# Down projections with tile 2's activations in two slots, the residual added by VectorE, and probability splits placed behind the next exponentials

## The chip, the cores and the metric

The kernel runs on one core of a Trainium2 chip. The metric is the device time of one execution in microseconds (us), lower being better; several executions are timed and their median is compared.

The core has engines that each work through their own instructions in order: TensorE (PE in the profile, with its weight loads as PEld), VectorE (DVE), ScalarE (ACT), GpSimd (POOL) and SyncE (SP), which here only starts DMA transfers. They wait for each other by semaphores.

## The reference

A block of four layers is applied to x of shape (2, 1024, 512) in fp32, each with a layer norm ahead of it and x added after it:

```python
x = x + attn_a(layernorm(x))
x = x + ffn(layernorm(x))
x = x + attn_b(layernorm(x))
x = x + ffn(layernorm(x))
```

attn_a is a chunked linear attention with 4 heads of 128 and chunks of 128; the change does not touch it. attn_b is a softmax attention of one head of width 512, without a mask, over 2 batches of 1024 rows, with weights W_q, W_k, W_v, W_o:

```python
scores = einsum('bqe,bke->bqk', Q, K) / sqrt(512)
out = einsum('bqk,bke->bqe', softmax(scores), V) @ W_o
```

ffn has a hidden width of 1408. Its weights are integers, W = (wq - 128) * scale per output column, and it computes `qlinear(silu(qlinear(x, gate)) * qlinear(x, up), down)`. Both ffn layers use the same weights.

## The kernel before

The 2048 rows of x are 16 tiles of 128 rows. A group is 4 tiles, so 512 rows. All matmuls are to be nearly as exact as fp32. For this, operands are split into a high part (rounded by a copy on ScalarE) and a low part (source minus high part, mostly on VectorE): `split`, lines 83 to 86, with the copy in L85 and the subtraction in L86. A product is then two or three matmuls of these parts that add up in PSUM (L96 to L98 in `mm3`).

The four layers run one after another: attention A, the ffn called "f" (L777), attention B, and the ffn called "g" (L959). What the next layer needs at its start (layer norm of its first groups, sums of operands for its first products) is done in steps that are placed among the work of the layer before.

**The ffn** (lines 670 to 775) runs in two halves, `pr` = 0 and 1, of 8 tiles each. In a half, a loop runs over the 11 blocks of 128 hidden columns, `j`. The gate and up products of the half's two groups are made by a Strassen scheme with seven block products instead of eight (`products`, L304, P1 to P7); their sums are put together on ScalarE and VectorE, and `finish` (L695 to L718) applies silu, multiplies gate by up, and writes the hidden activations: tiles 0 and 1 into a work tile `sg`, tiles 2 and 3 into `ha`, tiles 4 to 7 into `hb`. `finish` of block j is written after the first four products of block j+1; that of the last block stands behind the loop. `finish` also splits the block's part of tiles 0 and 1 into their `hs` tiles (128x128 elements; the subtraction is VectorE's in f's first half and for the last block, GpSimd's otherwise). An `hs` tile holds both parts of one row tile's whole hidden activation, 128 x 2 x 1408; they come from a pool with two buffers, so tile 2 can be split only when the projection of tile 0 has read its own, tile 3 when that of tile 1 has, and so on.

Behind the loop over j come the **down projections** of the 8 tiles, `i` = 0 to 7 (L747 to L775). Step i splits tile i+1 (L752, in two parts of 6 and 5 blocks, 768 and 640 elements wide), loads x of the tile into `xr` (SyncE, L754), makes 22 matmuls of 128x128 by 128x512, by turns with the high part (L761) and the low part (L762) of each hidden block, multiplies by the scale of the columns (VectorE, L763), adds x (L765, on GpSimd; on VectorE for the very last tile, which goes in two halves), and stores the tile (SyncE, L769). Then two of the side steps for the next half or layer are placed, ordered behind the last split of this step. At i = 4 the first half also loads the first two weight blocks of the second half (`stationary`, L775); the third follows when the next half begins. Weight blocks and the operands of the products lie in a pool "slots" of 12 tiles of 128 x 2048 (L39, function `slot`). A half has eleven weight blocks, made three ahead, and a slot is free again when the seven products of its block are done.

**Attention B** (lines 788 to 956) goes over the tiles `t` of queries. `scores_b` makes the scores in two PSUM tiles (psc), takes their maximum on VectorE (L829, with L832 and L833 to form `nm`), exponentials on ScalarE (L838, into `pe`, with their sum), and the reciprocal of the sum (`ri`, VectorE, L848 and L849). `probs_T` transposes the exponentials: VectorE transposes within blocks of 32 (L871), the result is stored to DRAM (L873), and four loads (L881) bring it back in transposed order to `ptl`. Then L884 to L886 split it in two parts, high parts into `pth`, low parts in place. Only for the last tile, t = 15, PE makes the transposes instead (ppt, L866), and their PSUM result is split at once. `out_b` makes 24 matmuls with the split V (pob, L96 to L98), scales by `ri` and adds x (L897), and stores (L898). The loop at the end of the stage calls, for each i, side steps, `scores_b` of i+1, `probs_T` of i, and `out_b` of i-1; after the loop it makes the first two weight blocks of ffn g and then `out_b` of tile 15.

**What sets the order.** The program is written in the order above, but the framework schedules it: a planner simulates the program and gives each engine its order, within the dependences and within edges that the kernel states. `behind(...)` states such edges: what is placed inside comes, on its own engine, after the instructions named. The list `last` holds the latest tile's two exponentials and reciprocal. A change of an edge or of an engine can therefore also move instructions far from the edited lines.

Of the kernel before, what the change touches and what calls it, by code (L numbers as in the profile page):

```python
# [10 lines left out]
F32R = mybir.dt.float32r  # L11
I32 = mybir.dt.int32
AF = mybir.ActivationFunctionType
ALU = mybir.AluOpType
AX = mybir.AxisListType

P = 128
# [7 lines left out]
KH = HID // P  # L25
ST = 4
# [8 lines left out]
def hybrid_block_kernel(ctx: ExitStack, tc: tile.TileContext, a, out):  # L35
    nc = tc.nc
# [12 lines left out]
    def slot(name, dt=F32R):  # L49

        return wp.tile([P, 2048], dt, tag="slot", name=name)
# [24 lines left out]
    def behind(inss):  # L76

        es = ExitStack()
        for ins in inss:
            es.enter_context(tc.issue_after(ins))  # L80
        return es

    def split(hi, lo, src, eng=None):

        c = nc.scalar.copy(hi, src)  # L85
        return c.ins, (eng or nc.vector).tensor_tensor(lo, src, hi.bitcast(F32), ALU.subtract).ins  # L86
# [583 lines left out]
    def ffn(src, dst, nm, wcs, after):  # L670


        with ExitStack() as fctx:
            fh = fctx.enter_context(tc.tile_pool(name=f"ffnh{nm}", bufs=1))
            f1 = fctx.enter_context(tc.tile_pool(name=f"ffn1{nm}", bufs=2))
            fw = fctx.enter_context(tc.tile_pool(name=f"ffnw{nm}", bufs=KH))
            fp = fctx.enter_context(tc.tile_pool(name=f"ffn{nm}", bufs=4))
            wd = []
            for pr in range(2):
                if pr == 0:  # L680
                    early = ln_steps(src, nm, 2) + ln_steps(src, nm, 3)
                    late = combine(nm, 1)
                else:
                    early, late = (list(x) for x in after)

                ha = fh.tile([P, 2, KH, P], F32, tag="ha", name=f"ha{nm}{pr}")
                hb = fh.tile([P, ST, KH, P], F32, tag="hb", name=f"hb{nm}{pr}")
                hs = {}

                def h_split(i, js, src, eng):  # L690
                    if i not in hs:
                        hs[i] = f1.tile([P, 2, KH, P], F32R, tag="hs", name=f"hs{nm}{pr}_{i}")
                    return split(hs[i][:, 0, js], hs[i][:, 1, js], src, eng)

                def finish(j, w, X, Z, V, up):  # L695

                    products(X, w, nm, pr, "P2", False)
                    products(Z, w, nm, pr, "P3", False)
                    products(V, w, nm, pr, "P4", False)
                    tiles = lambda x: x.rearrange("p (i c) -> p i c", c=P)  # L700
                    su = su_s[:, j : j + 1]
                    sg = fp.tile([P, 512], F32, tag="sg", name=f"sg{nm}{pr}_{j}")
                    nc.scalar.activation(sg, X, AF.Silu, scale=sg_s[:, j : j + 1])
                    nc.scalar.activation(hb[:, :, j], tiles(Z), AF.Silu, scale=sg_s[:, j : j + 1])
                    h01 = sg[:, 0:256]
                    nc.vector.scalar_tensor_tensor(h01, V[:, 0:256], su, h01, ALU.mult, ALU.mult)
                    nc.vector.scalar_tensor_tensor(
                        ha[:, :, j], tiles(V[:, 256:512]), su, tiles(sg[:, 256:512]), ALU.mult, ALU.mult
                    )
                    nc.vector.scalar_tensor_tensor(hb[:, :, j], tiles(up), su, hb[:, :, j], ALU.mult, ALU.mult)  # L710
                    for i in range(2):
                        done = h_split(
                            i,
                            j,
                            h01[:, i * P : (i + 1) * P],
                            None if j == KH - 1 or (nm == "f" and pr == 0) else nc.gpsimd,
                        )
                    return done  # L718

                begun = None  # L720
                for j in range(KH):
                    for n in range(len(wcs), min(j + 3, KH)):
                        wcs.append(stationary(n, f"{nm}{pr}", (xp, "xres") if nm == "f" and pr == 0 else None))
                    w = wcs[j]
                    X, Y, Z, V = (psum(f"p{n}{nm}{pr}_{j}") for n in "XYZV")
                    for ps, n in ((X, "P1"), (Y, "P6"), (Z, "P5"), (V, "P7")):
                        products(ps, w, nm, pr, n, True)
                    u2 = fp.tile([P, 512], F32, tag="sg", name=f"u2{nm}{pr}_{j}")
                    nc.scalar.copy(u2, X)  # L729
                    nc.vector.tensor_tensor(u2, Y, u2, ALU.add)  # L730
                    up = fp.tile([P, 512], F32, tag="sg", name=f"up{nm}{pr}_{j}")
                    nc.scalar.copy(up, Z)
                    nc.vector.tensor_tensor(Z, Z, u2, ALU.add)
                    nc.vector.tensor_tensor(V, V, u2, ALU.add)
                    nc.vector.tensor_tensor(up, V, up, ALU.add)  # L735
                    if begun:
                        finish(*begun)
                    begun = j, w, X, Z, V, up
                    for _ in range((1, 1, 1, 1, 2, 2, 1, 1, 1, 1, 2)[j] if early else 0):
                        early.pop(0)()  # L740
                    if pr == 0:
                        d = fw.tile([P, 512], F32R, tag="wd", name=f"wd{nm}{j}")
                        nc.sync.dma_start(out=d.bitcast(F32), in_=wd_d[j])
                        wd.append(d)
                done = finish(*begun)
                wcs = []
                for i in range(2 * ST):  # L747
                    t = pr * 2 * ST + i
                    if 1 <= i < 2 * ST - 1:
                        n = i + 1  # L750
                        for js in (slice(0, 6), slice(6, KH)):
                            done = h_split(n, js, ha[:, n - 2, js] if n < ST else hb[:, n - ST, js], None)  # L752
                    xr = xp.tile([P, D], F32, tag="xres", name=f"xr{nm}{t}")
                    nc.sync.dma_start(out=xr, in_=src[t])  # L754
                    o = fp.tile([P, 512], F32, tag="sg", name=f"o{nm}{t}")

                    last = nm == "g" and t == NT - 1
                    for ds in [slice(0, 256), slice(256, 512)] if last else [slice(0, 512)]:
                        ps = psum(f"po{nm}{t}_{ds.start}")[:, ds]
                        for j in range(KH):  # L760
                            nc.tensor.matmul(ps, hs[i][:, 0, j], wd[j][:, ds], start=j == 0, stop=False)  # L761
                            nc.tensor.matmul(ps, hs[i][:, 1, j], wd[j][:, ds], start=False, stop=j == KH - 1)  # L762
                        nc.vector.tensor_tensor(o[:, ds], ps, sd_b[:, ds], ALU.mult)  # L763
                        add = nc.vector if last else nc.gpsimd
                        add.tensor_tensor(xr[:, ds], o[:, ds], xr[:, ds], ALU.add)  # L765
                        if last:
                            nc.sync.dma_start(out=dst[t][:, ds], in_=xr[:, ds])
                    if not last:
                        nc.sync.dma_start(out=dst[t], in_=xr)  # L769
                    with behind(done):  # L770
                        for _ in range(2 if i > 0 else 0):
                            if early or late:
                                (early or late).pop(0)()
                    if pr == 0 and i == 4:
                        wcs = [stationary(n, f"{nm}1") for n in range(2)]  # L775
# [12 lines left out]
    with ExitStack() as bctx:  # L788
# [3 lines left out]
        for dst, d, n in ((wm, m_d, "wm"), (wvo, vo_d, "wvo")):  # L792
            two = [slot(f"{n}{m}") for m in range(2)]
# [58 lines left out]
        def probs_T(b, i):  # L852
# [4 lines left out]
            if t == NT - 1:  # L857

                lo = bp.tile([P, NK, P], F32R, tag="ptl", name=f"ptl{t}")
                hi = bp.tile([P, NK, P], F32R, tag="pth", name=f"pth{t}")  # L860
                for s in range(2):
                    ps = psum(f"ppt{t}_{s}").rearrange("p (k c) -> p k c", k=4)
                    ks = slice(s * 4, s * 4 + 4)
                    for k in range(4):
                        n = (s * 4 + k) * P
# [10 lines left out]
            lo = bp.tile([P, NK, P], F32R, tag="ptl", name=f"ptl{t}")  # L876
            hi = bp.tile([P, NK, P], F32R, tag="pth", name=f"pth{t}")
            raw = lo.bitcast(F32)
            placed = p_d[i].rearrange("k (c j) (r q) -> r j (k c) q", c=4, r=4)
            for r in range(4):  # L880
                nc.sync.dma_start(  # L881
                    out=raw[32 * r : 32 * (r + 1)].rearrange("p k (c q) -> p (k c) q", c=4), in_=placed[r]
                )
            for s in range(2):  # L884
                ks = slice(s * 4, s * 4 + 4)
                split(hi[:, ks], lo[:, ks], raw[:, ks])  # L886
            ptT[t] = hi, lo, ri

        def out_b(b, i):
# [132 lines left out]
```

## Time and profile before

| | |
|---|---|
| time, median of 3 runs | 997.01 us (995.41 to 999.16) |
| profiled execution | 995.43 us |
| its span in the trace | 993.7 us |
| mean clock of TensorE | 0.991 of full |
| busy: PE, DVE, ACT, POOL | 955.3, 681.8, 374.2, 269.0 us |
| L765 on GpSimd, ffn f and g | 16 of 25.0 us in all, 15 of 24.4 us in all |
| matmuls L761 and L762, f | 176 and 176 |
| matmuls L761 and L762, g | 187 and 187 |

The profile is of one execution. The span runs from its first instruction to its last; the execution's own time lies a little above it. Times are in microseconds from the span's start; "ns" is said where it is meant. A group's row names line, engine, operation, output, inputs, sizes and count; after the first bar stand busy time and mean length in ns, after the second the idle time of that engine just before these instructions, and what ended most of it. A row of the timeline starts with the start and the length of one instruction or of several that follow each other, and ends with the wait ahead of it in brackets. The letters f, g and b at the end of names stand for the two ffn layers and for attention B: `hsf`, `pof` and `xrf` are hs, the projection's PSUM tile and xr of ffn f. Successive matmuls of 512 columns start 0.227 us apart at full clock; a matmul's own length in the rows is longer, since they overlap.

### The profile page before, as it was taken

What the parts mean: (1) busy time and instruction counts of PE and PEld (TensorE: products, weight loads), DVE (VectorE), ACT (ScalarE), POOL (GpSimd) and SP (SyncE); (2) the same over time, 40 slices, a digit from 0 to 9 for tenths busy, and PEclk for the clock granted to TensorE, in tenths of its full rate; (3) what the DMA queues carried; (4) which work ended last, traced back from release to release, by engine and by line L of the source; (5) the groups of instructions that cost most, each with busy time, mean ns of one, the idle gap of its engine ahead of it and who ended that gap; (6) DMA issues with size and microseconds to landing.
All of it is one profiled execution on the core that took longest, in us unless ns stands there. A gap on an engine that the chain in (4) does not pass through costs nothing.

```text
span 993.7 us, 13137 instructions
## 1 busy us (share of the span) xinstructions
PE 955.3 (96%) x4450; PEld 786.8 (79%) x4450; DVE 681.8 (69%) x1294; ACT 374.2 (38%) x719; POOL 269.0 (27%) x345
## 2 busy tenths in 40 slices
PE   8999999988898999999999999999997999999998
PEld 6788888877776777887888888888876888788877
DVE  7666858779876699786526556356667775976665
ACT  4653334233665433443222223222223443444421
POOL 4442314253634133212200411205501111321122
PEclk9999999999999999999999999999998999999999
DMA  8536364564797555652704767328668762464112
GB/s 271 200 104 174 124 156 140 142 180 158 253 350 229 148 202 205 185 146 75 264 22 88 163 162 168 98 64 190 165 151 271 250 175 44 152 235 153 38 53 96
DMA packets 219250, 160.06 MB, mean 161 GB/s; under 512 B 154992, under 2 KB 170672, under 8 KB 219184
## 3 DMA queue, kind: packets, MB, share of 16 engines
q1 hardware_dynamic: 217136, 155.03, 52.3%
q0 software_dynamic: 2048, 4.20, 2.0%
q8 instruction: 35, 0.57, 0.2%
q14 instruction: 31, 0.25, 0.1%
HBM read 102.66 MB, written 41.84 MB: 145 GB/s over the span
## 4 chain that ended last, share of the span: by engine, by line
PE 56%; DVE 2%; SPq 2%; DMA 1%; ACT 1%; issue 1%; POOL 0%; ACTq 0%; DVEq 0%
PE pZg L304 4%; PE pXg L304 4%; PE pVg L304 4%; PE pog L762 4%; PE pog L761 4%; PE psc L96 3%; PE psc L98 3%; PE pob L96 3%; PE psc L97 3%; PE pob L97 3%; PE pob L98 3%; PE pYg L304 2%; PE pof L762 2%; PE pof L761 2%; PE pqb L97 1%; PE pqb L96 1%
## 5 line engine op out<-in xcount | busy, mean ns | idle before, releaser
L762 PE MATMUL pof<-wdf,hsf 128*128 128x512 f32 x176 | 68.3, 392 | 4.3 <-DVE hsf L86 4.3
L762 PE MATMUL pog<-wdg,hsg 128*128 128x512 f32 (+1 forms) x187 | 69.0, 378 | 3.0 <-DVE hsg L86 3.0
L761 PE MATMUL pog<-wdg,hsg 128*128 128x512 f32 (+1 forms) x187 | 69.1, 378 | 0.0
L761 PE MATMUL pof<-wdf,hsf 128*128 128x512 f32 x176 | 68.1, 391 | 0.0
L96 PE MATMUL pob<-vh,pth 128*128 128x512 f32 x128 | 50.8, 397 | 0.0
L96 PE MATMUL psc<-xh_b,qh 128*128 128x512 f32 x128 | 50.5, 395 | 0.0
L98 PE MATMUL psc<-xh_b,ql 128*128 128x512 f32 x128 | 50.5, 395 | 0.0
L97 PE MATMUL psc<-xT_b,qh 128*128 128x512 f32 x128 | 50.5, 394 | 0.0
L97 PE MATMUL pob<-vl,pth 128*128 128x512 f32 x128 | 50.5, 394 | 0.0
L98 PE MATMUL pob<-vh,ptl 128*128 128x512 f32 x128 | 50.4, 394 | 0.0
L304 PE MATMUL pXf<-B_f,wcf 128*128 128x512 f32 x176 | 47.0, 395 | 3.3 <-ACT u2f L729 2.2
L86 POOL TENSOR_TENSOR hsg<-sgg,hsg 128x128 fp32r<-128x128 f32 x40 | 17.6, 460 | 117.6 <-ACT hsg L85 95.4
L304 PE MATMUL pVf<-T_f,wcf 128*128 128x512 f32 x176 | 46.6, 391 | 1.4 <-DVE upf L735 0.7
L304 PE MATMUL pXg<-B_g,wcg 128*128 128x512 f32 x176 | 47.2, 389 | 0.0
L304 PE MATMUL pVg<-T_g,wcg 128*128 128x512 f32 x176 | 46.7, 389 | 0.0
L85 ACT CAST pth<-ptl 128x512 fp32r<-128x512 f32 x30 | 17.1, 619 | 75.9 <-DMA ptl<-p 64.0
L765 POOL TENSOR_TENSOR xrf<-of,xrf 128x512 f32<-128x512 f32 x16 | 25.0, 1562 | 75.3 <-DVE of L763 61.4
L838 ACT ACTIVATE pe<-psc,nm 128x512 f32<-128x512 f32 x32 | 21.7, 684 | 58.6 <-DVE nm L833 58.6
L762 PEld LDWEIGHTS pog<-wdg,hsg 128*128 128x128 f32 x187 | 35.1, 188 | 10.0 <-DVE hsg L86 3.6
L762 PEld LDWEIGHTS pof<-wdf,hsf 128*128 128x128 f32 x176 | 33.1, 188 | 12.6 <-DVE hsf L86 5.8
L304 PEld LDWEIGHTS pXf<-B_f,wcf 128*128 128x128 f32 x176 | 32.3, 188 | 12.8 <-ACT u2f L729 4.0
L765 POOL TENSOR_TENSOR xrg<-og,xrg 128x512 f32<-128x512 f32 x15 | 24.4, 1624 | 61.5 <-DVE og L763 48.7
(288 smaller groups left out, 2667.7 us busy)
## 6 DMA issues: line engine op xcount, KB each, us to landing
wcg<-wc SPq DMA_DIRECT2D x22, 896.0 KB, 5.8
wc<-wcf SPq DMA_DIRECT2D x11, 896.0 KB, 4.5
wcf<-wc SPq DMA_DIRECT2D x11, 896.0 KB, 4.8
p<-py SPq DMA_DIRECT2D x15, 512.0 KB, 3.0
ptl<-p SPq DMA_DIRECT2D x60, 128.0 KB, 3.0
xin_a<-in_x SPq DMA_DIRECT2D x16, 256.0 KB, 4.6
xra<-in_x SPq DMA_DIRECT2D x16, 256.0 KB, 3.0
row<-cl SPq DMA_DIRECT2D x16, 256.0 KB, 4.0
```

The lines of the kernel that those rows point to most:

```text
L85: c = nc.scalar.copy(hi, src)
L86: return c.ins, (eng or nc.vector).tensor_tensor(lo, src, hi.bitcast(F32), ALU.subtract).ins
L96: nc.tensor.matmul(ps, lhs_hi, rhs_hi, start=first, stop=False)
L97: nc.tensor.matmul(ps, lhs_hi, rhs_lo, start=False, stop=False)
L98: return nc.tensor.matmul(ps, lhs_lo, rhs_hi, start=False, stop=last).ins
L304: nc.tensor.matmul(ps, w[:, m, k * P : (k + 1) * P], o[:, s, k, :], start=first and k == 0 and s == 0, stop=k == 1 and s == 1, skip_group_ ...
L761: nc.tensor.matmul(ps, hs[i][:, 0, j], wd[j][:, ds], start=j == 0, stop=False)
L762: nc.tensor.matmul(ps, hs[i][:, 1, j], wd[j][:, ds], start=False, stop=j == KH - 1)
L765: add.tensor_tensor(xr[:, ds], o[:, ds], xr[:, ds], ALU.add)
L838: nc.scalar.activation(pe[:, s * 512 : (s + 1) * 512], pS[s], AF.Exp, bias=nm, scale=SC, accum_out=rs[:, s : s + 1],).ins
```

## The change

Four things are edited.

- Tile 2 of each half gets its high and low parts in two tiles of the pool "slots" instead of an `hs` tile, and is split before `finish` of the last block (blocks 0 to 9) and right after it (block 10). With that, `hs[i]` is a pair of views, and the matmuls name them accordingly.
- The splits in the loop of the down projections run two tiles ahead: step i, for i = 1 to 5, splits tile i+2. The side steps of these i stand behind that split.
- The addition of x (L765) is always done by VectorE.
- In `probs_T`, the two splits of each tile but the last are placed behind `last`, which at that point holds the exponentials and the reciprocal of the tile after it.

```diff
@@ -689,8 +689,14 @@
                 def h_split(i, js, src, eng):
                     if i not in hs:
-                        hs[i] = f1.tile([P, 2, KH, P], F32R, tag="hs", name=f"hs{nm}{pr}_{i}")
-                    return split(hs[i][:, 0, js], hs[i][:, 1, js], src, eng)
+                        if i == 2:
+                            two = [slot(f"hs{nm}{pr}_{i}{n}") for n in "hl"]
+                            hs[i] = [x[:, 0 : KH * P].rearrange("p (j c) -> p j c", j=KH) for x in two]
+                        else:
+                            both = f1.tile([P, 2, KH, P], F32R, tag="hs", name=f"hs{nm}{pr}_{i}")
+                            hs[i] = both[:, 0], both[:, 1]
+                    hi, lo = hs[i]
+                    return split(hi[:, js], lo[:, js], src, eng)
@@ -742,12 +748,14 @@
+                h_split(2, slice(0, KH - 1), ha[:, 0, 0 : KH - 1], None)
                 done = finish(*begun)
+                h_split(2, KH - 1, ha[:, 0, KH - 1], None)
                 wcs = []
                 for i in range(2 * ST):
                     t = pr * 2 * ST + i
-                    if 1 <= i < 2 * ST - 1:
-                        n = i + 1
+                    if 1 <= i < 2 * ST - 2:
+                        n = i + 2
                         for js in (slice(0, 6), slice(6, KH)):
                             done = h_split(n, js, ha[:, n - 2, js] if n < ST else hb[:, n - ST, js], None)
@@ -758,11 +766,10 @@
-                            nc.tensor.matmul(ps, hs[i][:, 0, j], wd[j][:, ds], start=j == 0, stop=False)
-                            nc.tensor.matmul(ps, hs[i][:, 1, j], wd[j][:, ds], start=False, stop=j == KH - 1)
+                            nc.tensor.matmul(ps, hs[i][0][:, j], wd[j][:, ds], start=j == 0, stop=False)
+                            nc.tensor.matmul(ps, hs[i][1][:, j], wd[j][:, ds], start=False, stop=j == KH - 1)
                         nc.vector.tensor_tensor(o[:, ds], ps, sd_b[:, ds], ALU.mult)
-                        add = nc.vector if last else nc.gpsimd
-                        add.tensor_tensor(xr[:, ds], o[:, ds], xr[:, ds], ALU.add)
+                        nc.vector.tensor_tensor(xr[:, ds], o[:, ds], xr[:, ds], ALU.add)
@@ -881,9 +888,10 @@
-            for s in range(2):
-                ks = slice(s * 4, s * 4 + 4)
-                split(hi[:, ks], lo[:, ks], raw[:, ks])
+            with behind(last):
+                for s in range(2):
+                    ks = slice(s * 4, s * 4 + 4)
+                    split(hi[:, ks], lo[:, ks], raw[:, ks])
             ptT[t] = hi, lo, ri
```

## The prediction

> **What bounds the kernel now.** I read the busy shares first, then TensorE's waits by line, then each of those places in the timeline, then busy time by stretch. The page's first line:
>
> ```profile
> PE 955.3 (96%) x4450; PEld 786.8 (79%) x4450; DVE 681.8 (69%) x1294; ACT 374.2 (38%) x719; POOL 269.0 (27%) x345
> ```
>
> TensorE (PE) is busy for 955.3 of 993.7 us. The change takes no matmul away (4450 stay), so it can return only idle time of PE, at most 38 us, and of that only what its edits touch. The waits of PE (us in total, times, longest):
>
> ```profile
> PE ppt L866 <- ACT pe L838: 6.8, 1, 6.8
> PE pof L762 <- DVE hsf L86: 4.3, 4, 1.5
> PE pog L762 <- DVE hsg L86: 3.0, 2, 1.5
> PE pVf L304 <- DVE of L763: 0.7, 1, 0.7
> ```
>
> These 14.8 us are all that the edits can reach: two kinds of stall in the down projections, and one at the end of attention B. The timeline at the start of the second half of FFN f (start, length, engine) shows the first kind:
>
> ```profile
> 459.20 2.82 ACT L85 CAST hsf<-haf 128x768 fp32r<-128x768 f32 x4 [4.88 <-PE pof L762]
> 459.91 1.28 POOL L765 TENSOR_TENSOR xrf<-of,xrf 128x512 f32<-128x512 f32 x1 [9.63 <-DVE of L763]
> 460.07 1.93 DVE L86 TENSOR_TENSOR hsf<-haf,hsf 128x768 fp32r<-128x768 f32 x1 [0.24 <-ACT hsf L85]
> 462.06 0.50 PE L762 MATMUL pof<-wdf,hsf 128*128 128x512 f32 x1 [1.47 <-DVE hsf L86]
> ```
>
> Tile 2's split can begin only when tile 0 has left its buffer (two buffers), while PE already works on tile 1. ScalarE copies at 459.20, VectorE subtracts at 460.07, and PE, which wanted tile 2's low half at 460.32 (its high half began at 460.09, and matmuls start 0.227 us apart), gets it at 462.06: 1.74 us lost. The subtraction took 1.93 us, while the same size takes 0.94 us where no add of POOL lies beside it (355.60). Over all tiles:
>
> ```profile
> L86 DVE TENSOR_TENSOR hsf<-haf,hsf 128x768 fp32r<-128x768 f32 x4 | 8.0, 2001 | 0.4 <-ACT hsf L85 0.4
> L86 DVE TENSOR_TENSOR hsg<-hag,hsg 128x768 fp32r<-128x768 f32 x4 | 8.0, 2004 | 0.5 <-ACT hsg L85 0.5
> ```
>
> All eight first parts took 2.0 us: POOL's add stands beside every one. The third place is the end of attention B:
>
> ```profile
> 748.12 1.14 ACT L85 CAST pth<-ptl 128x512 fp32r<-128x512 f32 x2 [8.83 <-DMA ptl<-p]
> 749.16 1.99 ACT L85 CAST T_g<-xT_g 128x1024 fp32r<-128x1024 f32 x2
> 751.06 0.68 ACT L838 ACTIVATE pe<-psc,nm 128x512 f32<-128x512 f32 x1
> 751.88 1.97 PE L866 MATMUL ppt<-ident,pe 128*128 128x128 f32 x8 [6.79 <-ACT pe L838]
> ```
>
> ScalarE does its work in order. The copies of tile 14's transposed probabilities wait 8.83 us for a DMA, and the last tile's exponentials (L838) stand behind them and behind two casts, so PE idles 6.8 us. By stretch (PE, PEld, DVE, ACT, POOL busy; clock; DMA), the four down projections are:
>
> ```profile
> 344.00:390.00 46.00, 42.45 (x184) 33.77 (x183) 41.77 (x55) 17.57 (x23) 16.22 (x12) 1.00 0.57 198
> 459.00:490.00 31.00, 29.53 (x130) 24.04 (x129) 24.96 (x27) 12.85 (x20) 9.20 (x7) 1.00 0.66 237
> 845.00:882.00 37.00, 35.53 (x156) 29.01 (x155) 34.30 (x32) 16.49 (x21) 12.30 (x8) 1.00 0.51 171
> 957.00:988.00 31.00, 29.47 (x144) 24.57 (x143) 21.42 (x20) 8.38 (x12) 11.13 (x7) 1.00 0.32 106
> ```
>
> In f's first half VectorE is busy 91% (41.77 of 46), in g's first half 93%: there it is nearly a bound itself. I call the four f0, f1, g0, g1.
>
> **What the Trainium skill says.** (1) "SBUF — State Buffer", section "Who interferes with whom": a VectorE instruction with two SBUF inputs and a GpSimd instruction reading SBUF cannot overlap; the first to issue holds the shared port pair for its whole length. The trace agrees: 1.93 against 0.94 us above. (2) "VectorE: DVE Perf Modes", section on the TRN2 errata: an fp32 tensor_tensor runs at one element per cycle, 691 ns by its formula for 512. The trace has 680 ns for the xT_b subtractions of 512 (L86). (3) "GPSIMD Engine Reference", its table of speeds: tensor_tensor is about twice as slow on GpSimd. The trace: 1.28 us undisturbed against 0.68. (4) "TensorE: Matmul & The Clock Gate", Part 1: after an idle window of about 3.4 us the clock is halved. Here it is at half from 750.07 to 756.90, after the 6.8 us idle; the stalls of 1.5 us cost no clock.
>
> **The change part by part.** *Tile 2 in two slots.* It removes the wait for tile 0's buffer. Ten of its eleven blocks are split ahead of the last finish: one copy of 128x1280 on ScalarE, about 1.3 us (scaled from 0.84 for 768), and one subtraction on VectorE, 1.4 us (1280 elements at 0.94/768 each, less the fixed part). The cover is idle time just there, 1.8 to 2.1 us on ScalarE and about 3 on VectorE while they wait for PE's last products; without it each would delay finish, and so the first projection, by 1.4 us. The slots it takes held weight blocks 8 and 9, which are read for the last time before that, so nothing waits for them; that the tile gets no slot in time is thereby ruled out. It issues no DMA. Gain: the four stalls of tile 2, 1.76 (f0), 1.74 (f1), 1.74 (g0), 1.80 (g1) = 7.0.
>
> *Splits two tiles ahead.* Tiles 3 and 4 then have two projections' time (2 x 22 x 0.227 = 10 us), and from tile 5 on one (5.0 us) for 1.5 us of copies and 1.75 us of subtractions. The copies and subtractions are as many as before. In f0 two later stalls, 1.25 and 0.40, fall under this. After the splits of tile 7 at i=5 there is no further one, so the side steps (norm and combine of the next stage, their loads on SP among them) are tied to no later split.
>
> *Adds on VectorE.* 31 adds leave POOL, 49.4 us by its two rows, with nobody on PE's path behind them. On VectorE each costs about 0.61 us (start to start of the 0.68 row): 31 x 0.61 = 19 us. It gets back the blocking: each 768 or 640 subtraction of the tables above (and some of the next stage's) loses about 1.0 to 1.1 us: 5.0 in f0, 5.4 in f1, 6.3 in g0, 6.6 in g1, 23 in all. Net -4 us of VectorE work, none of it on the path by itself. By half: f0 8 x 0.61 = 4.9 against 5.0, so VectorE keeps its 41.8 us, while PE, with its gaps closed, would want the stretch in 41.8. So in f0 VectorE is level with PE and the queue at the seam to f1 matters: the add of each tile now stands in VectorE's order, and SP's store of that tile, and behind it the load of the next x and of the third weight block of f1, wait for it. Price at the seam: 0 (all hidden) to 2 us, I take 1.0 for f1's first products waiting on VectorE's split of f1's operand, and 0.35 for the weight block (issue about 381, landing 4.5 to 5.8 us later, needed at about 386.2). Against it the present wait of 0.85 at 387.80 (pVf behind L763) goes. f0: 1.76+1.25+0.40+0.85-1.35 = 2.9 (range 1 to 4.3). In f1 and g0 the same queues have 2 to 3 us to spare, in g1 nothing follows: 1.74, 1.74, 1.80.
>
> *Splits behind the exponentials.* No instruction is added; two copies and two subtractions per tile go behind the next tile's exponentials on ScalarE, and behind its reciprocal on VectorE. What they held up was pe15: it now starts once its own maximum is there and pe14 is through. Tile 14's exponentials also stood behind a copy: it ran at 735.22 with its nm ready at 730.37. So pe15 comes at about 746 to 748. What is late next: the order of PE after the change is the transposes of tile 15, four matmuls on high halves, then the low half of tile 14, whose subtraction now stands behind tile 15's reciprocal and the norm and combine steps of g. Among them is one that waits for a load which follows a store. I work it out at 753 to 753.9. From there 44 matmuls remain, 44 x 0.227 = 10.0, plus 0 to 1.2 for the clock (an idle of 2 to 4 us may or may not halve it): 763.0 to 765.1, against 766.08 now. I take 763.8, a gain of 2.3 (range 0.5 to 5). Elsewhere in attention B PE has no such wait: an output is formed two score tiles later than its split, and there the move costs and gains nothing; if that cover failed it would be 1.3 us for each of 14 tiles.
>
> Sum: 2.9 + 1.74 + 2.3 + 1.74 + 1.80 = 10.5 us. Span 993.7 - 10.5 = 983.2; the profiled execution took 995.43 (1.7 us outside the span), so 984.9 for such a run. It was the quick end of the runs (median 997.01, 995.41 to 999.16), so I set 997.0 - 10.5 = 986.5.
>
> **The rivals.** *Half the gain.* VectorE stays the bound in f0 and the tail gains nothing because tile 14's low half is as late as now: only f1, g0, g1, 5.3 us, time 991.7. For: 91% busy there. Against: the blocking that goes is as large as the adds that come.
>
> *The whole idle time.* Tile 14's low half comes early, the idle of 6.8 us and the half clock (8 matmuls at 0.43 instead of 0.227: 1.6 us) both go: 8.4 instead of 2.3, 16.6 us in all with f0 as forecast, or some less: 981. Against: VectorE is busy all 6.83 us of that stretch.
>
> *Slower: SP's queue behind VectorE's adds.* The adds sit in VectorE's order behind norm and combine steps; the store of a tile waits for its add, and the next stage's weights (896 KB, 5.8 us to landing) for the store. If stores slip by one projection (5.0 us), the weights come 5, 3 and 2 us late at f0's, f1's and g0's seams (margins 0, 2, 3): 10, and all is level, 996.5. Above one tile's slip it decides: one and a half give 7.5+5.5+4.5 = 17.5 and 1004. For: f0's VectorE has no slack. Against: its work there doesn't grow.
>
> **How the numbers follow.** About 0.5% (5 us) is what a measurement of this kernel can tell from no change. Forecast (8 to 13 us) 0.60; half the gain 0.22, on the limit of 5 us, so 0.11 faster and 0.11 same; whole idle 0.10; SP's queue 0.08 (0.03 same, 0.05 slower). Faster 0.81, same 0.14, slower 0.05. The range runs from the whole idle (981) past half the gain to 993, and leaves out the queue and the edges.
>
> **What would show it.** Right: no wait of pof or pog at L762 on hsf/hsg in f1, g0, g1; 768-wide subtractions near 0.95 us; pe15 before 749; first matmul of g0 near 763.8. Wrong: PE waiting for a DMA of wcf, wcg or wm at a seam; a wait of pob on ptl that ends after 755; finish of the last block later by the split put ahead of it.

## The result: no change, and the profile after

In 12 runs of each kernel the changed one took 997.96 us in the median (993.29 to 1002.06), the one before 997.82 (993.89 to 999.55): a ratio of 1.0000 with an interval of 0.9981 to 1.0019. The forecast of 986.5 us and its range of 981 to 993 were missed: what can be measured is no change.

The profiled execution of the changed kernel took 993.29 us (span 991.6). It was the quickest of its 12 runs, so its waits are, if anything, shorter than usual. The first line of its page, and its waits of PE:

```profile
PE 958.5 (97%) x4450; PEld 788.5 (80%) x4450; DVE 677.7 (68%) x1325; ACT 374.5 (38%) x719; POOL 221.6 (22%) x314
```

```profile
PE ppt L873 <- ACT pe L845: 5.5, 1, 5.5
...
PE pZf L304 <- DVE pZf L739: 2.8, 3, 1.5
...
PE pob L96 <- ACT pth L85: 1.4, 2, 1.1
...
PE pXf L304 <- DMA wcf<-wc: 0.8, 1, 0.8
...
PE pob L98 <- DVE ptl L86: 0.5, 1, 0.5
...
PE pof L770 <- DVE hsf L86: 0.3, 1, 0.3
```

The 31 adds have left POOL for DVE (1325 instructions instead of 1294, 314 instead of 345), and DVE is nevertheless busy for less (677.7 instead of 681.8). The waits of the projections on hs, 4.3 and 3.0 us before, are down to 0.3. New in their place are pXf behind a weight block's DMA, pob behind both halves of the probabilities, and a longer wait of pZf on VectorE.

The starts of the same matmuls in both traces, taken stage by stage, show where the time went (us):

| stage, by first matmuls | before | after | predicted |
|---|---|---|---|
| f0: its first projection to the 32nd pXf of f1 | 69.96 | 69.40 | -2.9 |
| f1: its first projection to attention B's first scores | 65.43 | 63.68 | -1.74 |
| attention B, first scores to the end of tile 13's output | 231.02 | 232.61 | 0 |
| its end, from there to the last output matmul | 21.15 | 22.75 | -2.3 |
| g0: its first projection to the 32nd pXg of g1 | 66.09 | 64.35 | -1.74 |
| g1: from there to the last projection | 89.43 | 87.62 | -1.80 |

f1, g0 and g1 came as forecast to a hundredth. f0 gave 0.6 instead of 2.9, and attention B lost 3.2 instead of gaining 2.3. The rows of f0 and g0 end on a product some way into the next half, so that what is lost at the seam between the halves is in them.

**The seam of f's halves.** The trace of after there, first PE, then SP's queue (start, length):

```profile
388.23 1.20 PE L304 MATMUL pZf<-B_f,wcf 128*128 128x512 f32 x4 [1.48 <-DVE pZf L739]
390.26 0.97 PE L304 MATMUL pXf<-B_f,wcf 128*128 128x512 f32 x3 [0.83 <-DMA wcf<-wc]
```

```profile
381.15 0.32 SPq L776 DMA_DIRECT2D x<-xrf  x1
383.83 0.32 SPq L762 DMA_DIRECT2D xrf<-x  x1
384.24 0.38 SPq L106 DMA_DIRECT2D xin_b<-x  x1
384.67 0.90 SPq L293 DMA_DIRECT2D wcf<-wc  x2
```

SP issues the store of tile 6 at 381.15. Next in its queue stands the load of x for tile 8, into one of two buffers, and it has to wait until that store has landed (383.81). Only behind it, and behind a load for attention B, comes the third weight block, at 384.67. It lands at 390.21, and PE is already there. In the kernel before, SP's queue at this place had another order:

```profile
375.03 0.32 SPq L769 DMA_DIRECT2D x<-xrf  x1
377.05 0.32 SPq L754 DMA_DIRECT2D xrf<-x  x1
377.43 0.42 SPq L293 DMA_DIRECT2D wcf<-wc  x1
383.14 0.32 SPq L769 DMA_DIRECT2D x<-xrf  x1
...
386.35 0.42 SPq L754 DMA_DIRECT2D xrf<-x  x1
```

There the third weight block (377.43, landed 382.07) stood ahead of the store of tile 6 (383.14) and of the load of x for tile 8 (386.35). Counted from f0's first projection, it was issued after 45.2 us, in the changed kernel after 51.2.

**The end of attention B.** ScalarE, VectorE and PE of after:

```profile
747.86 1.99 ACT L85 CAST T_g<-xT_g 128x1024 fp32r<-128x1024 f32 x2 [7.50 <-DVE xT_g L245]
749.76 0.68 ACT L845 ACTIVATE pe<-psc,nm 128x512 f32<-128x512 f32 x1
...
751.09 1.13 ACT L85 CAST pth<-ptl 128x512 fp32r<-128x512 f32 x2
```

```profile
748.59 0.14 DVE L840 TENSOR_SCALAR nm<-nm 128x1 f32<-128x1 f32 x1
...
754.72 1.27 DVE L86 TENSOR_TENSOR ptl<-ptl,pth 128x512 fp32r<-128x512 f32 x2
```

```profile
750.58 1.97 PE L873 MATMUL ppt<-ident,pe 128*128 128x128 f32 x8 [5.47 <-ACT pe L845]
...
753.71 0.79 PE L96 MATMUL pob<-vh,pth 128*128 128x512 f32 x1 [0.30 <-ACT pth L85]
...
755.45 0.79 PE L98 MATMUL pob<-vh,ptl 128*128 128x512 f32 x1 [0.52 <-DVE ptl L86]
```

Tile 14's copies have indeed gone behind tile 15's exponentials. But these start at 749.76, because their nm is only there at 748.73 and two casts for g stand ahead of them. Then PE waits twice more, for tile 14's high and low parts, and it does so at half clock: the output matmuls are 0.43 us apart up to 759.9 (in the kernel before, up to 756.6).

### The profile page after: what moved, and what is told of

Read it like the earlier page. It is cut to its first block, busy times and chain, and to the rows that moved or that the text cites. A ratio compares the mean times of both kernels' runs of the same rounds, so it can differ in the third digit from the quotient of the medians.

```text
span 991.6 us, 13092 instructions
## 1 busy us (share of the span) xinstructions
PE 958.5 (97%) x4450; PEld 788.5 (80%) x4450; DVE 677.7 (68%) x1325; ACT 374.5 (38%) x719; POOL 221.6 (22%) x314
## 4 chain that ended last, share of the span: by engine, by line
PE 58%; DMA 8%; DVE 5%; ACT 1%; issue 1%; SPq 1%; POOL 1%; DVEq 0%; ACTq 0%; POOLq 0%
PE pog L770 4%; PE pog L769 4%; PE pVg L304 4%; PE pXg L304 4%; PE pZg L304 4%; PE pof L770 2%; PE pof L769 2%; PE pVf L304 2%; PE pZf L304 2%; PE pob L98 2%; PE pXf L304 2%; PE psc L96 2%; PE psc L98 2%; PE psc L97 2%; PE pob L96 2%; PE pob L97 2%
## 5 line engine op out<-in xcount | busy, mean ns | idle before, releaser
L769 PE MATMUL pog<-wdg,hsg 128*128 128x512 f32 (+1 forms) x165 | 60.3, 375 | 0.0
L770 PE MATMUL pog<-wdg,hsg 128*128 128x512 f32 (+1 forms) x165 | 60.2, 375 | 0.0
L770 PE MATMUL pof<-wdf,hsf 128*128 128x512 f32 x154 | 59.7, 392 | 0.4 <-DVE hsf L86 0.3
L769 PE MATMUL pof<-wdf,hsf 128*128 128x512 f32 x154 | 59.3, 389 | 0.0
L114 POOL TENSOR_TENSOR rs_b<-ve_b,mhalf 128x1 f32<-128x1 f32 x16 | 12.6, 788 | 207.9 <-DVE ve_b L112 181.9
L836 DVE TENSOR_REDUCE mx<-psc 128x1 f32<-128x512 f32 x32 | 21.8, 685 | 26.4 <-PE psc L98 26.2
L304 PEld LDWEIGHTS pVf<-T_f,wcf 128*128 128x128 f32 x176 | 32.9, 188 | 8.1 <-DVE upf L741 1.4
L304 PEld LDWEIGHTS pXg<-B_g,wcg 128*128 128x128 f32 x176 | 33.1, 188 | 6.9
L304 PEld LDWEIGHTS pVg<-T_g,wcg 128*128 128x128 f32 x176 | 33.1, 188 | 6.9
```

What stands on the lines that cost most here:

```text
L114: nc.gpsimd.tensor_tensor(rs, ve, mhalf, ALU.pow)
L304: nc.tensor.matmul(ps, w[:, m, k * P : (k + 1) * P], o[:, s, k, :], start=first and k == 0 and s == 0, stop=k == 1 and s == 1, skip_group_ ...
L769: nc.tensor.matmul(ps, hs[i][0][:, j], wd[j][:, ds], start=j == 0, stop=False)
L770: nc.tensor.matmul(ps, hs[i][1][:, j], wd[j][:, ds], start=False, stop=j == KH - 1)
L836: nc.vector.tensor_reduce(mx[:, s : s + 1], ps, AX.X, ALU.max)
```

## The experiments

All times are medians; the kernel before ran beside each group (997.5, 998.1, 998.2 and 997.8 us), and ratios are against it. Two columns of a table further down give what each profile shows of f0 and of the end of attention B.

**The change without its last part.** The splits of the probabilities stand as before:

```diff
-            with behind(last):
-                for s in range(2):
+            for s in range(2):
```

> The change without its last part: the splits of the probabilities stand as before, not behind the next exponentials; slots for tile 2 and adds on VectorE stay. My theory (the three down projections f1, g0, g1 give 5.3 us, f0 about 0.6, and the end of attention B gives 3.2 back because its matmuls run at half clock with waits in between): the first product of g comes about 3 us earlier against the last scores than with the whole change, span about 988, 5 to 6 us faster than before (0.995). Rival 1 (the end of attention B is lost to other things, such as the extra VectorE adds ahead of it): no faster than the whole change. Rival 2 (a profile does not stand for the timed runs and the gains are not real): within 2 us of before.

Measured: 995.98 us, 0.9986 (0.9972 to 1.0000). That is 2.0 us less than the whole change took, but the two intervals overlap, so this pair alone doesn't show that the last part costs. Of the 5 to 6 us of gain expected, 1.5 came. The theory fell short in one place, which the profile shows. In this execution f0 took 74.38 us, 5 more than in the profile of the whole change, though f's instructions stand in the same order in both:

```profile
386.10 0.32 SPq L776 DMA_DIRECT2D x<-xrf  x1
389.42 0.32 SPq L762 DMA_DIRECT2D xrf<-x  x1
389.84 0.38 SPq L106 DMA_DIRECT2D xin_b<-x  x1
390.27 0.90 SPq L293 DMA_DIRECT2D wcf<-wc  x2
```

```profile
393.18 1.20 PE L304 MATMUL pZf<-B_f,wcf 128*128 128x512 f32 x4 [1.48 <-DVE pZf L739]
397.98 1.22 PE L304 MATMUL pXf<-B_f,wcf 128*128 128x512 f32 x2 [3.61 <-DMA wcf<-wc]
```

It is the same queue as above, but the store took 3.3 us to land and the weight block 7.7, and PE waited 3.61 us for it. Behind that wait the clock was at half from 397.95 to 401.36, and the next eight matmuls took 3.50 us instead of 1.82, a loss of 1.7 us more. What looked like a small wait in one profile is a varying one. From here on the theory was that f0's slots lose at this seam what they gain before it.

**The last part alone** (the same edit on the kernel before):

> The last part alone: only the splits of the probabilities are placed behind the next exponentials. My theory: about 3 us slower than before (1.003), all of it between tile 12's output and the first product of g: a wait of 1.2 us of an output on its high halves near 728, the idle ahead of the last transposes 5.5 instead of 6.8, and more matmuls at half clock after it. Rival (the loss there came with the slots and adds): same as before or up to 2 us faster.

Measured: 999.90 us, 1.0022 (1.0009 to 1.0035). The last part alone makes the kernel slower. Its size is as expected; the profile of one execution (the quickest of 22) does not show it, its end of attention B being 2 us shorter than before.

**The slots alone**, with the adds on POOL:

```diff
-                        nc.vector.tensor_tensor(xr[:, ds], o[:, ds], xr[:, ds], ALU.add)
+                        add = nc.vector if last else nc.gpsimd
+                        add.tensor_tensor(xr[:, ds], o[:, ds], xr[:, ds], ALU.add)
```

> Tile 2 in two slots and splits two tiles ahead, but x is added by GpSimd as before, and the splits of the probabilities stand as before. Theory: the slots alone take the four stalls of tile 2 away (7.0 us), since the split then has time even when a GpSimd add blocks it; in f0 the subtractions stay at 2 us, so later stalls and the seam cost up to 2 us. Span about 987 to 989, 5 to 7 us faster than before. Rival (the adds on VectorE are what frees the subtractions in time): stalls of up to 1 us stay at several tiles, gain under 3 us.

Measured: 994.73 us, 0.9977 (0.9964 to 0.9989). The stalls of f1, g0 and g1 are gone as with the adds moved (63.68, 64.35 and 87.62 us), so the slots alone do that, and in these three halves the rival is out. The gain is under 3 us all the same, 2 to 4 less than expected, and again it is f0 that misses. f0 took 71.15 us, 1.2 more than before, and 2.1 more for the same work, since in this kernel's order four matmuls (0.9 us) fewer lie between the two marks. At the seam pZf waits 2.6 us for VectorE, and the clock is at half behind it (393.6 to 397.0). Although the adds are on POOL here, the third weight block is issued late, at 390.62, behind the store of tile 7 as well.

**The adds alone** (L765 always on VectorE, nothing else):

> Only the adds of x move to VectorE; tile 2 still waits for tile 0's buffer, splits one tile ahead. Theory: the subtraction of 768 falls from 2.0 to about 0.95 us, so each of the four stalls of tile 2 shrinks from 1.75 to about 0.7 us (4 us in all), f0's later stalls go, and f0's seam takes up to 2 us: 2 to 4 us faster than before. Rival (what delays tile 2 is the buffer alone): stalls stay at about 1.7 us, no gain.

Measured: 990.36 us in 6 runs, 0.9928 (0.9905 to 0.9952), more than expected. Each of the four stalls of tile 2 fell from 1.75 to 1.1 us, and f0 took 67.29 us instead of 69.96, without any wait at the seam. Since the slots with the adds had given only 1.5 us, the theory was that the slots do harm somewhere. The next two split them.

**Slots in all halves but f0**, and **slots in f0 only**, both with the adds on VectorE and without the last part:

```diff
+                ahead = 2 if (nm, pr) != ("f", 0) else 1
...
-                        if i == 2:
+                        if i == 2 and ahead == 2:
...
-                    if 1 <= i < 2 * ST - 2:
-                        n = i + 2
+                    if 1 <= i < 2 * ST - ahead:
+                        n = i + ahead
```

The two splits ahead of and behind the last finish stand under `if ahead == 2`; the second kernel has `==` for `!=` in the first line.

> Adds on VectorE everywhere; tile 2 in two slots and splits two tiles ahead in f's second half and in both halves of g, but f's first half as in the kernel with only the adds moved; splits of the probabilities as before. My theory (the slots pay in three halves and cost in f's first half, where PE's filled gaps only turn into waits at the seam on VectorE and on a weight block): the 990.4 of the adds alone less three stalls of 1.13 us, about 987 (0.989). Rival (the low time of the adds alone came from few lucky runs, and the slots do no harm in f's first half): about 994 to 996, like the change without its last part.

> The complement: slots and splits two ahead only in f's first half; adds on VectorE everywhere; splits of the probabilities as before. Theory: f's first half loses by the slots, so this is slower than the adds alone by 3 to 7 us, 994 to 999, with waits of pZ on VectorE and of pX on wcf at the seam of f's halves that the adds alone do not have. Rival (no harm there): 990 or less.

Measured: 988.65 us, 0.9914 (0.9882 to 0.9946), and 999.04 us, 1.0013 (0.9992 to 1.0033). The loss by the slots in f0 is clear against the adds alone (0.9928). The gain in the other three halves is 1.1 us each in the profiles; the timed runs, 0.9914 against 0.9928, are too few to show it. In f0 only, the profile has both waits again:

```profile
PE pXf L304 <- DMA wcf<-wc: 3.2, 1, 3.2
...
PE pZf L304 <- DVE pZf L740: 2.8, 3, 1.5
```

and f0 took 74.07 us, with the clock at half from 392.8 to 399.6; without slots there it took 68.29.

**Operand sums of g later**, on the kernel with only the adds:

```diff
-            fill[1][(5, 5, 5, 5, 5, 6, 6, 6, 6, 7, 7, 7)[n]].append(step)
+            fill[1][(5, 5, 5, 5, 5, 7, 7, 7, 7, 7, 7, 7)[n]].append(step)
```

> Only the adds on VectorE, and the four sums of operands for g that attention B makes at its seventh query tile move to its eighth, so that the last tile's maximum and nm have fewer VectorE steps ahead of them. Theory of the tail (VectorE's queue, not the ScalarE copies, makes the last exponentials late): the last transposes start 3 to 6 us earlier against the last scores, the idle falls from 5.6 to under 3 us, and the time falls by 1 to 4 us against the adds alone: 987 to 989. Rival (the steps moved are late for g's first products): the gain is given back there, 990 to 993.

Measured: 999.01 us, 1.0009 (0.9991 to 1.0027). Both were right in part, and both missed the time. The idle ahead of the last transposes fell from 5.4 to 0.7 us, so it is VectorE's queue ahead of nm that made the last exponentials late, not only ScalarE's copies. But g's first product then waited 8.3 us for its weights, where the rival had expected the gain to be given back and no more:

```profile
PE pXg L304 <- DMA wcg<-wc: 8.3, 1, 8.3
```

```profile
761.00 0.32 SPq L897 DMA_DIRECT2D x<-xrb  x1
763.19 0.79 SPq L743 DMA_DIRECT2D wdg<-wd  x2
764.03 1.06 SPq L293 DMA_DIRECT2D wcg<-wc  x2
```

The scheduler had put the weight loads behind the store of tile 14, which waits for its output, so they could not start before 761. It is the same trap as at f's seam, with other names.

**The adds and the last part**:

> Adds on VectorE, and the splits of the probabilities behind the next exponentials; tile 2 as before. Theory: the last part costs about 2 us wherever it stands (0.9986 against 1.0 with slots and adds, 1.0022 alone), so 992 to 993. Rival (its cost comes from one chance of order in those two kernels): 990 or less.

Measured: 994.76 us, 0.9981 (0.9966 to 0.9995), slower than the adds alone: the last part costs on this base too.

**The third weight block asked for early**, on the change without its last part:

```diff
-                        wcs = [stationary(n, f"{nm}1") for n in range(2)]
+                        wcs = [stationary(n, f"{nm}1") for n in range(3 if nm == "f" else 2)]
```

> The change without its last part, and f's first half asks for the third weight block of its second half together with the first two, so that its load stands on SP's queue ahead of the stores that wait for VectorE's adds. Theory (of what the slots cost in f's first half, one part is SP's queue: the block's load waits behind the store of tile 6 and the next load of x; the other part is VectorE at the seam): the wait of pX on wcf at the seam (1.0 to 3.8 us in three profiles) goes, the wait of pZ on VectorE (1.6) stays; 2 to 4 us faster than the change without its last part, so 992 to 994. Rival (the load is late because of the memory traffic, not the queue): the wait stays within 1 us.

Measured: 989.65 us, 0.9909 (0.9878 to 0.9941), 6.3 us faster by one line than the change without its last part, more than expected. The three loads now start at 368.57, ahead of the stores. Both waits are gone, also the one on VectorE that was to stay. PE at the seam:

```profile
388.92 1.07 PE L304 MATMUL pVf<-T_f,wcf 128*128 128x512 f32 x4
389.83 1.07 PE L304 MATMUL pXf<-B_f,wcf 128*128 128x512 f32 x4
390.74 1.07 PE L304 MATMUL pYf<-T_f,wcf 128*128 128x512 f32 x4
391.64 1.07 PE L304 MATMUL pZf<-B_f,wcf 128*128 128x512 f32 x4
```

Between pVf and pZf, where PE had stood for 1.48 us, there are now eight matmuls, pXf and pYf, of the third block. With its weights at hand, PE has something to do while VectorE catches up. So moving this one load took away both waits. f0 took 66.75 us; in this order, too, four matmuls fewer lie between the marks, so 67.7 for the same work. That is no less than with the adds alone. The line was not tried on a kernel without slots in f0; those have no wait on wcf at the seam.

**A version of what helped**: adds on VectorE, slots but not in f0, the operand sums later, and g's first two weight blocks asked for at i = 5 and 6 of the last batch instead of behind the loop:

```diff
+                if b + 1 == NB and i in (5, 6):
+                    wcs.append(stationary(len(wcs), "g0"))
...
-        wcs = [stationary(n, "g0") for n in range(2)]
```

> A version made of what helped: adds on VectorE, slots in all halves but f's first, splits of probabilities as before, the four operand sums of g moved from attention B's seventh to its eighth tile, and g's first two weight blocks asked for two and one tiles earlier, so that their loads do not stand behind the stores at the end. Theory: the idle ahead of the last transposes falls from about 4.5 to about 1 us and no half clock follows, without the 8.4 us wait on g's weights that the moved sums brought: 2 to 5 us faster than 988.65, so 984 to 987. Rival (the end of attention B is bound by VectorE's total work there, and the wait only moves to g's first operands): 988 to 990.

Measured: 985.65 us in 6 runs, 0.9862 (0.9835 to 0.9889): faster than both kernels. The transposes start 0.23 us after PE is ready and run at full clock (1.33 us for the eight, instead of 1.97), and no wait on wcg is left. The half clock did follow, though, from 748.25 to 751.66, behind waits of 0.23, 1.48 and 0.27 us:

```profile
743.68 1.33 PE L876 MATMUL ppt<-ident,pe 128*128 128x128 f32 x8 [0.23 <-ACT pe L848]
746.49 0.50 PE L96 MATMUL pob<-vh,pth 128*128 128x512 f32 x1 [1.48 <-ACT pth L85]
```

**The last part but for tile 14**, **the adds alone once more**, and **the last part for tile 14 only**, all with the adds on VectorE and tile 2 as before:

```diff
-            with behind(last):
+            with behind(last if t != NT - 2 else ()):
```

The third has `==` for `!=`.

> Adds on VectorE, splits of the probabilities behind the next exponentials for all tiles but the last pair (tile 14's split stands as before). Theory (what the last part costs is at tile 14: its copies and subtraction stand behind tile 15's exponentials and reciprocal, and the last outputs wait 0.7 and 1.0 us for them at half clock): as fast as the adds alone, 990 to 991. Rival (it costs along the whole of attention B): 993 to 995, as with all tiles.

> The kernel with only the adds moved, once more, since its time rests on six runs. Theory: 990 to 991 again. Rival (those runs were lucky): 993 to 995, and then the last part's cost and the slots' cost in f's first half are smaller than read so far.

> Adds on VectorE, and only tile 14's split of the probabilities behind the next exponentials. Theory (the end of attention B bears the cost: the last outputs wait for the high and low parts of tile 14, 0.7 and 1.0 us in every profile with the last part and in none without): 2 to 3 us slower than the adds alone, 993 to 995. Rival (the cost lies in the other tiles): 990.4 to 992, like the adds alone.

Measured: 994.06 us, 0.9960 (0.9945 to 0.9975); 992.02 us, 0.9936 (0.9909 to 0.9964), which agrees with the first 0.9928 within the intervals; and 991.57 us, 0.9942 (0.9922 to 0.9963). My theory, that the end of attention B bears the cost, fell: with tile 14 alone moved, the time is that of the adds. Its profile beside one of the adds alone shows a gain and a loss of the same size. ScalarE, with tile 14 moved, and then with the adds alone:

```profile
744.89 0.68 ACT L837 ACTIVATE pe<-psc,nm 128x512 f32<-128x512 f32 x1
...
746.23 1.13 ACT L85 CAST pth<-ptl 128x512 fp32r<-128x512 f32 x2
```

```profile
744.20 1.14 ACT L85 CAST pth<-ptl 128x512 fp32r<-128x512 f32 x2 [9.11 <-DMA ptl<-p]
...
747.14 0.68 ACT L837 ACTIVATE pe<-psc,nm 128x512 f32<-128x512 f32 x1
```

The exponentials come 2.25 us earlier, and PE's idle ahead of the transposes falls from 4.3 to 2.0 us. From the first transpose to g's first product it then takes 15.65 instead of 13.24 us: the outputs wait 0.5 us for tile 14's high part, and the clock is at half for 6.8 us (746.28 to 753.10) instead of 3.4. In these two executions, what is gained ahead of the transposes is given back behind them; how much of the longer half clock is chance is not shown.

**The whole change with the third weight block early** (the one line above):

> The whole change, and f's first half asks for the third weight block of its second half together with the first two. Theory (the place of that load on SP's queue took the gain of the slots and adds): both waits at the seam of f's halves, pZ on VectorE and pX on wcf, go, and it is 5 to 7 us faster than the whole change: 990.5 to 993 (0.993 to 0.995). Rival (its gain in e9 hung on the last part being left out): 995 to 998.

Measured: 993.67 us, 0.9950 (0.9934 to 0.9965), 4.3 us faster than the whole change, a little less than expected. No wait on wcf is left at the seam, and the one of pZf is gone; one of 0.4 us on VectorE is new. This profile, of the slowest of 17 runs, does not show where the 4.3 us lie: its f0 is no shorter than in the profile of the whole change, which was of the quickest of 12.

The two stages in which the kernels differ most, by profile (us), with the measured ratio:

| kernel | f0 | end of B | ratio |
|---|---|---|---|
| before | 69.96 | 21.15 | 1 |
| whole change | 69.40 | 22.75 | 1.0000 |
| without last part | 74.38 | 20.83 | 0.9986 |
| last part alone | 69.77 | 19.17 | 1.0022 |
| slots alone | 71.15* | 19.95 | 0.9977 |
| slots in f0 only | 74.07 | 18.90 | 1.0013 |
| slots not in f0 | 68.29 | 17.91 | 0.9914 |
| adds alone, both times | 67.29, 66.99 | 18.83, 17.70 | 0.9928, 0.9936 |
| adds and last part | 67.89 | 20.75 | 0.9981 |
| the same, but not for tile 14 | 67.43 | 19.53 | 0.9960 |
| the same, for tile 14 only | 67.62 | 17.79 | 0.9942 |
| whole change, third block early | 69.16* | 22.50 | 0.9950 |
| the same without last part | 66.75* | 21.61 | 0.9909 |

\* Four matmuls fewer lie between the marks; for the same work add 0.9 us.

## Why the prediction was wrong

**Tile 2 in slots, in f1, g0 and g1**: right. The stalls went, 1.75, 1.74 and 1.81 us by stage, and the subtraction of 1280, 1.49 us (1.4 forecast), was hidden ahead of the last finish.

**Adds on VectorE**: right in the balance. The subtraction of 768 takes 950 ns instead of 2000, as the rule of the Trainium skill on the shared port ("SBUF — State Buffer", "Who interferes with whom") would have it, and VectorE's total fell by 4.1 us (4 forecast). That by itself it was worth 6 to 7 us was not seen: it shortens the stalls of f1, g0 and g1 by 0.6 us each, and f0 as a whole by 2.7 to 3.0. The rest lies, in its two profiles, at the end of attention B, where PE's idle was 5.4 and 4.3 us instead of 6.8; whether the adds bring that is not shown.

**f0**: the step that failed is the 0.35 us for the third weight block, "issue about 381". At 381.15 the store of tile 6 went out, just as worked out. The load of x behind it then had to wait 2.7 us more for this store to land, since its buffer is that store's source, and the weight block stood behind both. The prediction names this order, but has no term for the landing. The block was issued at 384.67; with 5.5 to 7.7 us to landing, PE waited 0.8 to 3.6 us for it, and behind the waits of 3.2 and 3.6 us the clock fell to half as well.

It is the slots that put the block there. In the ten kernels without slots in f0 it stands ahead of the load of x for tile 8, in the four with them, and without the one line, behind it, with the adds on VectorE or on POOL. Why the scheduler orders it so is not shown. So f0's slots take 2.6 us of PE's gaps away (1.76, 1.25 and 0.40 before, 0.46 and 0.30 after), and bring PE sooner to a block that comes later. The second term, 1.0 us for VectorE at the seam, was 1.6; with the block early, the scheduler fills that wait too.

The rival "SP's queue behind VectorE's adds", given 0.08, had the right queue, but not the cause: the store was not late, and with the adds alone there is no wait at the seam. This is the largest single loss: 4.3 us on the whole change by one line, 6.3 without the last part.

**The end of attention B**: the idle did fall, by 1.3 us in the whole change and by 2.3 where tile 14 alone was moved, not by the 3 to 5 that a start at 746 to 748 meant: nm was late. The step that failed is "44 x 0.227 = 10.0, plus 0 to 1.2 for the clock". The half clock held for ten of those matmuls (2 us), and two waits, on tile 14's high part (0.3 us) and low part (0.5; 1.0 in two other profiles), fell into that time. I had only the second on the list, at 753 to 753.9; it ended at 755.45. So g's first product came at 767.71 instead of 763.0 to 765.1. With tile 14 alone moved, gain and loss cancel in the profiles, 2.3 against 2.4.

**"Elsewhere in attention B PE has no such wait"**: wrong in the profile of after, where tile 12's output waits 1.07 us for its high part; the other four profiles in which these tiles have the last part show no such wait. In timed runs the last part costs 2 to 4 us: 999.90 against 997.5 alone, 994.76 against 990.36 and 992.02 with the adds, 993.67 against 989.65 with the block early. With tile 14 left out the cost seems to stay (994.06 against 992.02 and 990.36), but the intervals overlap. The profiles show that margins shrink, not that they break. From the end of the copies of the high part to the first output matmul, tile 0 has 1.8 us instead of 7.8, tile 8 1.7 instead of 8.2, tile 13 2.5 instead of 6.9 (whole change against the second run of the adds alone); some other tiles keep theirs. If loads landed 2 us later in some executions, PE would then stop. This is argued, not shown: the profile of the kernel with the last part but for tile 14 has no wait in attention B, and where its 2 us lie stays open.

The sum of the profile: 0.6 + 1.75 - 3.2 + 1.74 + 1.81 = 2.7 us of gain in the changed stages, in the quickest of 12 executions. With f0 at 74.1 to 74.4, as in the two other profiles of the same f0, it would be a loss of 2; the median lies between. Without the last part and with the block early, the kernel was 8.6 us faster than before (5.9 to 12.2 by the interval), against 8.2 forecast for the other parts (2.9 + 1.74 + 1.74 + 1.80). So the two failed steps, the weight block's place and the last part, are enough to account for the miss. That this sum agrees is in part luck: with the block early, f0's slots bring nothing over the adds alone, and the adds bring more than was forecast for them.

## What to carry to other kernels

Before filling a stall of the busy engine, ask what it will need next, and where the load of that stands on the queue that issues it: a load behind a store waits for the store's source, and a load into the store's buffer waits until it has landed, so everything behind both is late by that landing time. An edit that names no DMA can move it there: here tile 2's new buffers did. Moving such a load a few places forward can be worth more than the stall; here one line was worth 4 to 6 us. And an edge that lets one piece of work go first makes another go second: price the second at the clock and with the margins that will be there then.

## What the runs showed that was not expected

One profile is not the kernel. Attention A, which no kernel touched, took from 251.9 to 257.1 us up to f's first product in the 16 profiles, and the same order of f's instructions had waits of 0.8 and of 3.6 us on one weight block. Stages that begin and end on the same matmuls could be compared to a hundredth of a us where no DMA is awaited (63.68 us in seven kernels), while whole spans could not be compared to within 5 us. Part of this is the clock: behind the idle at the end of attention B (waits of 4.0 to 7.6 us in all kernels but the two with the later sums and the one with tile 14 alone moved), between none and nine of the output matmuls were 0.43 us apart, and with no order in which longer idle means more of them. The Trainium skill, "TensorE: Matmul & The Clock Gate", Part 1, says that the window of the clock gate runs freely, so that the point of change depends on the moment; these runs agree. In all 16 traces the stretches at half clock begin on a grid of 3.41 us, each trace with its own offset, and last one, two or three steps of it (750.07 to 756.90 before, 749.76 to 760.00 after), save one that is cut off where the trace ends. An idle as long as such a step, as the prediction had it, is not needed: with tile 14 alone moved, the clock was halved at 746.28 behind an idle of 2.0 us.
